# A hybrid of scans, attention and mixtures: image 2's preparation beside image 3's first mixture, and scores without row maxima

## The chip, the cores and the metric

The kernel runs on one core of one Trainium2 chip, in one launch. The metric is the device time of that launch in microseconds (us). Engine names are those of the profile: PE is TensorE (matmuls), PEld its weight loads, DVE is VectorE, ACT is ScalarE, POOL is GpSimd, SP is SyncE, which here issues nearly all DMAs.

## The reference, cut to what matters

Four images of 32 x 32 positions (L = 1024 tokens) with C = 256 channels go through four layers.

```python
# layer 0: norm, project to 512, 3x3 depthwise conv, gelu, then a selective scan with N = 64 states
h = exp(dt[..., None] * A) * h + (dt * x)[..., None] * B[:, None, :]    # for each token in turn
y = einsum("bdn,bn->bd", h, C)
# layer 1: 1x1, grouped 3x3, 1x1 convolutions with a skip
# layer 2a: attention, 8 heads of 32, with a mask from edge_index
scores = where(mask, Q @ K.T / sqrt(32), -inf); attn = softmax(scores); out = attn @ V @ Wo + bo
# layer 2b: mixture of 8 experts (256 -> 256 -> 256), the top 2 of each token
# layer 3a: norm, project, silu, a selective scan with N = 16 states, gate, W_out
# layer 3b: mixture of 8 experts (256 -> 512 -> 256)
top2_vals, top2_idx = top_k(softmax(x @ gate_w + gate_b), 2)
out = sum over e of cw[:, e] * (gelu(x @ W1[e] + b1[e]) @ W2[e] + b2[e])
```

## The kernel before, in words

**Scans.** A scan works in units: one unit is 128 partitions (4 states of 32 channels) by 1024 tokens. There are 256 units an image in layer 0 and 64 an image in layer 3, 1280 in all, in the order (layer, image) = (0,0), (0,1), (3,0), (0,2), (0,3), (3,1), (3,2), (3,3). Each unit loads a tile of dt from memory (`dA<-dt`, 512 KB, on SP's queue, five buffers), takes its exponential on ACT, gets B spread over the partitions by two PE matmuls (`ps_rep`), multiplies on DVE (1.211 us), runs the scan instruction on DVE (2.284 us), multiplies by C on POOL, and is summed by PE (`ps_y`).

**Pacing.** Each engine carries out its instructions in the order in which the program wrote them. The program writes the units' instructions one half unit after another, and between them (`run`, `advance`) as many steps of the other work, a "side", as an estimate allows. `Metered` (line 138 is its `run`, hence the line of nearly every instruction in the profile) adds an estimated cost for each instruction to a clock of each engine, with `matmul_us` for matmuls; side steps are written as long as no engine's clock is ahead of VectorE's, at most two for each half unit. So a changed estimate moves instructions even where nothing else changes.

**Sides.** For each image the side is: the front of layer 0 (beside an earlier scan), then `middle` (the back of layer 0, layer 1, attention, the layer-2 mixture, the front of layer 3), then `last` (the back of layer 3 with `back3`, and the layer-3 mixture `moe(3, ...)`). Attention of one image runs beside the scan of another: image 3's runs beside (3,1) and (3,2).

**Attention.** `heads` works in 64 steps an image: (half of the queries, pair of heads, 128 keys). A step's `scores` are three kinds of matmul into the same PSUM tile `ps_sc`: the products kT by qT, then `onesb` (ones, 32 partitions) by `mT`, then the identity by `maskT`; ACT takes the exponential, and `values` multiplies it by v and by ones (the sums). `mT` holds, for each query and head, minus a row maximum. It is zero unless a bound on the scores, worked out in `attention`, is too large for the exponential: then the rarely taken branch of `shift` works the maxima out with `row_max`. When a group of heads is finished (four times an image), `divided` divides by the sums: DVE takes the reciprocal, POOL multiplies.

**The last layer's mixture.** Image 0's is dense. Images 1 to 3 are sorted: `moe(3, b, ...)` normalizes, routes, ranks the tokens by expert, scatters them (16 indirect DMAs on POOL) into piles of 256 rows in memory, and leaves; `piles` works all piles through (for each, `gx` transposes, `ps_h`, `ps_e`, and a store to `results`), and `gathered` collects each token's two rows and adds them to the image's running sum `tb`. Each image's preparation is `back3` (gate, the projection `ps_o` by W_out into `tb`) and the routing.

**Their places.** Three helpers set the order, and they are what the change touches. `beside(main, other)` writes one step of `other` after each step of `main`. `first_sorted` prepares image 1 beside image 3's layer-2 mixture, yields END, and later, as `self.other` in `last`, works through the piles. `rest` finishes what `other` has left up to END, and only then comes `front3` of image 3, ahead of the scan (3,3). `then_sorted` prepares image 2 and then image 3; `favour` mixes it with the piles, so image 2's preparation is written among the units of (3,3), and what of image 3's follows its scan stands behind the last unit.

Of the kernel before, what the change touches and what calls it, by code (L numbers as in the profile page):

```python
# [9 lines left out]
F32 = mybir.dt.float32  # L10
# [74 lines left out]
def matmul_us(out, lhsT=None, rhs=None, **_):  # L85
    if lhsT is None:
        lhsT = out
    us = 0.46e-3 * columns(out)
    if lhsT.dtype != BF16:
        us = max(4 * us, 0.3)  # L90
    if out.shape[0] <= 32:
        return us / 4
    return us / 2 if lhsT.shape[0] <= 32 else us


def by_columns(per, fixed, of=0):
# [53 lines left out]
class Hybrid:  # L150
# [1154 lines left out]
    def attention(self, b, tb):  # L1305
        nc, tc, vec = self.nc, self.tc, self.vec
        with tc.tile_pool(name=f"at{b}", bufs=1, side="right") as op:
            xa = op.tile([P, TB, C], F32, name="xa")
            qT = op.tile([P, 2, L], F32, name="qT")
            kT = op.tile([P, 2, L], F32, name="kT")  # L1310
            v = op.tile([P, TB, C], F32, name="v")
            mT = op.tile([P, 2, L], BF16, name="mT")
            maskT = op.tile([P, TB, L], BF16, name="maskT")
            wo = self.weight(op, "L2_attn_Wo", 2)
            large = op.tile([1, 1], I32, name="large")
            nc.vector.memset(mT, 0.0)
            with tc.tile_pool(name=f"aa{b}", bufs=1, side="right") as fp:
                wq, wk, wv = (self.weight(fp, "L2_attn_" + n, 2) for n in ("Wq", "Wk", "Wv"))
                xT = fp.tile([P, 2, L], F32, name="xTa")
                yield from self.norm(fp, tb, TB, xa, "lnt")  # L1320
                yield from self.turned(xa, TB, xT)

                def project(item):
                    w, dst, bias, sc, c, g = item
                    ps = self.ps("ps_qk")
                    cols = slice(g * 512, (g + 1) * 512)
                    self.mm(ps, lambda k: w[:, k, c * P : (c + 1) * P], xT, 2, cols)
                    nc.scalar.activation(
                        dst[:, c, cols], ps, AF.Identity, bias=bias[:, c : c + 1], scale=sc
                    )  # L1330

                yield from self.pipe(
                    [
                        (w, dst, bias, sc, c, g)
                        for w, dst, bias, sc in (
                            (wq, qT, self.bq, self.isq), (wk, kT, vec["L2_attn_bk"], 1.0)
                        )
                        for c in range(2) for g in range(2)
                    ],
                    project, cost=1.7,  # L1340
                )

                yield from self.large_scores(fp, qT, kT, large)
                for _ in self.mask_work:
                    pass
                nc.sync.dma_start(maskT, self.mem[("maskT",)].rearrange("j p f -> p j f"))

                def values(j):
                    ps = self.ps("ps_v", (P, 2, C))
                    for i in range(2):  # L1350
                        m = 2 * j + i
                        for k in range(2):
                            nc.tensor.matmul(
                                ps[:, i, :], lhsT=xT[:, k, m * P : (m + 1) * P], rhs=wv[:, k, :],
                                start=(k == 0), stop=(k == 1),
                            )
                    nc.scalar.copy(v[:, 2 * j : 2 * j + 2, :], ps)

                yield from self.pipe(range(TB // 2), values, cost=1.7)
            go = nc.values_load(large, engines=self.sides, min_val=0, max_val=1)  # L1360
            tc.mark_branch_hint_location(f"large{b}", go, engines=self.sides)
            yield from self.add_rows(xa, self.bo, TB)
            yield from self.add_rows(tb, self.beta, TB)
            with tc.tile_pool(name=f"ab{b}", bufs=1, side="right") as fp:
                yield from self.shift(fp, qT, kT, mT, maskT, go, f"large{b}")
            with tc.tile_pool(name=f"ac{b}", bufs=1, side="right") as fp:
                yield from self.all_heads(b, fp, tb, qT, kT, v, maskT, mT, xa, wo)

    def all_heads(self, b, fp, tb, qT, kT, v, maskT, mT, xa, wo):
        nc = self.nc  # L1370

        def divided(raw, sums, c):
            nc.vector.reciprocal(sums[:, c, :], sums[:, c, :])
# [8 lines left out]
            [fp.tile([P, 2, 512], F32, tag=t, name=t, bufs=2) for t in ("raw", "sums")]  # L1382
            for _ in range(2)
        ]
        scores, values = self.heads(fp, halves, qT, kT, v, maskT, mT)
        for n in range(len(steps) + 2):
            if n >= 2:
                values(steps[n - 2])
                yield 1.3
            if n < len(steps):  # L1390
                scores(steps[n])
                yield 1.3
            if then:
                more = next(then[0], None)
                if more is None:
                    then.pop(0)
                else:
                    yield more
            nh, hp, kb = steps[n - 2]
            if n >= 2 and kb == TB - 1 and hp % 2:  # L1400
                then.append(divided(*halves[nh], hp // 2))
                if nh == 0 and hp == 3:
                    then.append(self.finished(b, fp, tb, 0, halves[0][0], xa, wo, "s"))
# [40 lines left out]
        nc.vector.tensor_copy(large, most[:, 0:1])  # L1444
        yield 0.5

    def shift(self, fp, qT, kT, mT, maskT, go, label):


        nc, tc = self.nc, self.tc  # L1450
        clock = dict(self.clock)
        with tc.If(go, preferred_fallthrough_block=True, label=label):
            for _ in self.row_max(fp, qT, kT, mT, maskT):
                pass
        self.clock.update(clock)
        yield 1.0

# [58 lines left out]

        yield from self.pipe([(c, g) for c in range(2) for g in range(2)], turn, cost=0.8)

    def heads(self, fp, halves, qT, kT, v, maskT, mT):

# [4 lines left out]
        def scores(step):  # L1527
            nh, hp, kb = step
            qs = slice(nh * 512, (nh + 1) * 512)
            c, at = hp // 2, 64 * (hp % 2)  # L1530
            alone = self.alone
            if alone:
                both = self.scan_psum.tile([P, 2, 512], F32, tag="x", name="ps_sx", bufs=2)
                two = [both[:, i, :] for i in range(2)]
# [3 lines left out]
            for i in range(2):  # L1538
# [1 line left out]
                    two[i], lhsT=kT[rows[i], c, kb * P : (kb + 1) * P], rhs=qT[rows[i], c, qs],  # L1540
                    start=True, stop=False,
                )
            for i in range(2):
                nc.tensor.matmul(
                    two[i], lhsT=self.onesb[rows[i], :], rhs=mT[rows[i], c, qs],
                    start=False, stop=False,
                )
# [113 lines left out]
                self.router[which].rearrange("p k e -> p (k e)"), ps[:, : 2 * NEXP]  # L1661
            )

    def moe(self, which, b, tb, side="right", stack=None):

        nc, tc, a = self.nc, self.tc, self.a
        w1, w2, b1, hidden = (
# [6 lines left out]
        with ExitStack() as own:  # L1674
# [2 lines left out]
            xT = None if few else xp.tile([P, 2, L], F32, name="xTm")  # L1677
            cw = xp.tile([P, TB, NEXP], F32, name="cw")
            weights, op = {}, None
            spots = self.spots(xp) if few else None  # L1680

            def expert_weights(e):
                we1 = op.tile([P, 2, hidden], F32, tag="we1", name="we1", bufs=2)
# [431 lines left out]
    def gathered(self, b):  # L2115

        nc = self.nc
        tb, _, slot, share = self.sorted_of[b][:4]
        results, got = self.mem["results", b], {}

        def gather(j):
# [316 lines left out]
    def middle(self, b):  # L2438

        with self.tc.tile_pool(name=f"t{b}", bufs=1, side="right") as tp:  # L2440
# [3 lines left out]
            if b < NB - 1:  # L2444
                yield from self.attention(b, tb)
                yield from self.moe(2, b, tb)
            else:
                yield from self.attention(b, tb)
                self.other = self.first_sorted()
                yield from self.rest((yield from self.beside(self.moe(2, b, tb), self.other)))  # L2450
            yield from self.front3(b, tb)

    def some(self, other, n):
        for _ in range(n):
            yield next(other)

    def beside(self, main, other, begin=lambda: True):

        held = None
        for cost in main:  # L2460
            yield cost
            if other is None or not begin() or (held and held not in self.done):
                continue
            held = None
            more = next(other, END)
            if more is END:
                other = None
            elif isinstance(more, Wait):
                held = tuple(more)
            else:  # L2470
                yield more
        if held:
            yield Wait(held)
        return other
# [7 lines left out]
    def first_sorted(self):  # L2482

        with ExitStack() as stack:
            tb = self.scan_pool.tile([P, TB, C], F32, tag="rows", name="tb_rows", bufs=2)
            yield from self.back3(SORTED, tb, "left")
            yield from self.until("route", NB - 1)
            yield from self.moe(3, SORTED, tb, "left", stack)
            yield END
            op = stack.enter_context(self.tc.tile_pool(name="piles", bufs=1, side="left"))  # L2490
            yield from self.piles(op)
# [1 line left out]

    def then_sorted(self):

        with ExitStack() as stack:
            for b in range(SORTED + 1, NB):
                pool = stack.enter_context(self.tc.tile_pool(name=f"e{b}", bufs=1, side="right"))
                tb = pool.tile([P, TB, C], F32, name="tb")
                yield from self.back3(b, tb)  # L2500
                if b == NB - 1:
                    self.gather_pool = stack.enter_context(
                        self.tc.tile_pool(name="found", bufs=1, side="right")
                    )
                yield from self.moe(3, b, tb, "right", stack)
            while "written" not in self.passed:
                yield 0.0

# [77 lines left out]
```

## Time and profile before

Three runs took 6139.52, 6158.01 and 6163.36 us; the median is 6158.01. The profiled execution took 6153.73 us, with a span of 6152.0 us in the profile.

| stretch (us from the span's start) | what runs |
|---|---|
| 0 to 124 | set-up, front of layer 0 of image 0 |
| 124 to 5293 | the scans (0,0) to (3,2), one after another, about 1.3 us apart |
| 1430 to 1679, 2493 to 2740, 3859 to 4117, 4903 to 5149 | the heads of images 0 to 3, each beside a scan |
| 5002 to 5293 | scan (3,2), 291.6 us |
| 5293 to 5522 | no scan: rest of image 3's layer-2 mixture, with image 1's routing; front of (3,3); 228.6 us |
| 5523 to 5861 | scan (3,3), 337.7 us, beside the piles and image 2's preparation |
| 5861 to 6152 | tail, 291.3 us: end of image 3's preparation, the other piles, the gathers |

How to read it: a stretch's bound is the engine whose busy time fills the stretch, or the wait that ends last in it. The total busy share of an engine is an average over all of them. Matmuls on different row groups overlap, so a mean duration times a count can be more than the busy time.

### The profile page before, as it was taken

What the parts mean: (1) busy time and instruction counts of PE and PEld (TensorE: products, weight loads), DVE (VectorE), ACT (ScalarE), POOL (GpSimd) and SP (SyncE); (2) the same over time, 40 slices, a digit from 0 to 9 for tenths busy, and PEclk for the clock granted to TensorE, in tenths of its full rate; (3) what the DMA queues carried; (4) which work ended last, traced back from release to release, by engine and by line L of the source; (5) the groups of instructions that cost most, each with busy time, mean ns of one, the idle gap of its engine ahead of it and who ended that gap; (6) DMA issues with size and microseconds to landing.
All of it is one profiled execution on the core that took longest, in us unless ns stands there. A gap on an engine that the chain in (4) does not pass through costs nothing. (4 is left out here: it accounts for less than half of the span.)

```text
span 6152.0 us, 58992 instructions
## 1 busy us (share of the span) xinstructions
PE 4839.5 (79%) x19373; PEld 1936.7 (31%) x19373; DVE 5037.2 (82%) x4022; ACT 3253.7 (53%) x4225; POOL 3889.2 (63%) x2016
## 2 busy tenths in 40 slices
PE   6676777579979657988868987988865797887787
PEld 2121221032234203224414533224311322543476
DVE  5869798998899899889988998888989888526822
ACT  3455566335568534557754764557753455236431
POOL 1778677766577765657786775657786666306523
PEclk7686877579979757998977988988975897888798
DMA  3665555644345556634554564434555666238656
GB/s 110 187 189 174 155 173 161 201 140 145 124 144 194 164 185 160 162 119 150 198 177 153 173 209 138 133 115 149 197 181 163 164 159 170 74 103 220 175 179 190
DMA packets 396351, 993.17 MB, mean 161 GB/s; under 512 B 42020, under 2 KB 162417, under 8 KB 394417
## 3 DMA queue, kind: packets, MB, share of 16 engines
q1 hardware_dynamic: 388544, 973.48, 52.3%
q0 software_dynamic: 6896, 15.25, 0.9%
q8 instruction: 160, 2.62, 0.2%
q14 instruction: 175, 1.43, 0.1%
q10 hardware_dynamic: 576, 0.39, 0.0%
HBM read 869.33 MB, written 122.26 MB: 161 GB/s over the span
## 5 line engine op out<-in xcount | busy, mean ns | idle before, releaser
L138 POOL TENSOR_TENSOR h<-h,rows 128x1024 f32<-128x1024 f32 x1280 | 3030.0, 2371 | 1685.9 <-DVE h L138 1433.0
L138 DVE TENSOR_TENSOR_SCAN h<-dA,ps_rep 128x1024 f32<-128x1024 f32 x1280 | 2923.7, 2284 | 208.6 <-ACT dA L138 82.6
L138 DVE TENSOR_TENSOR ps_rep<-ps_rep,rows 128x1024 f32<-128x1024 f32 x1280 | 1549.8, 1211 | 205.4 <-PE ps_rep L138 195.3
L138 PE MATMUL ps_rep<-S,spread_L_conv_A_log 96*128 96x512 bf16 x2048 | 769.1, 466 | 843.3 <-DVE h L138 791.8
L138 ACT ACTIVATE dA<-dA,A_L_conv_A_log 128x1024 f32<-128x1024 f32 x1024 | 1126.4, 1143 | 531.9 <-DMA dA<-dt 502.6
L138 PE MATMUL ps_y<-h,collect_L_conv_A_log 128*32 128x512 f32 x4096 | 733.2, 761 | 37.2 <-POOL h L138 36.7
L138 PEld LDWEIGHTS <-spread_L_conv_A_log 96*128 96x128 bf16 x2048 | 159.6, 103 | 1651.5 <-DVE h L138 1329.2
L138 PE MATMUL ps_e<-we,h_m 128*128 128x256 f32 x2112 | 494.7, 385 | 9.0 <-ACT h_m L138 8.2
L138 ACT ACTIVATE p<-ps_sc 128x512 f32<-128x512 f32 x512 | 277.9, 594 | 405.1 <-PE ps_sc L138 400.3
L138 PEld LDWEIGHTS ps_e<-we,h_m 128*128 128x128 f32 x2112 | 402.2, 192 | 115.0 <-ACT h_m L138 25.5
L138 ACT ACT_TABLE_LOAD x326 | 418.3, 1283 | 21.1 <-DMA dA<-dt 15.1
L138 PE MATMUL ps_h<-xTm,we 128*128 128x512 f32 x768 | 366.3, 607 | 0.1
L138 ACT ACTIVATE dA<-dA,A_L_attn_A_log 128x1024 f32<-128x1024 f32 x256 | 283.1, 1144 | 143.4 <-DMA dA<-dt 122.2
L138 PE MATMUL ps_rep<-S,spread_L_attn_A_log 96*128 96x512 bf16 x512 | 182.6, 445 | 171.8 <-DVE h L138 145.1
L138 PE MATMUL ps_sc<-qT,kT 32*128 32x512 f32 x1024 | 310.3, 656 | 5.7 <-ACT p L138 2.4
L138 PE MATMUL ps_at<-p,v 128*32 128x512 f32 x1024 | 273.2, 614 | 0.0
L138 PE MATMUL ps_at<-p,ones 128*32 128x512 f32 x1024 | 273.2, 614 | 0.0
L138 PE MATMUL ps_cv<-pad,diag 128*128 128x512 f32 x504 | 235.1, 607 | 0.0
L138 PEld LDWEIGHTS ps_y<-h,collect_L_conv_A_log 128*32 128x32 f32 x4096 | 96.2, 119 | 376.4 <-issue 226.2
L138 ACT ACTIVATE h_m<-ps_h,cols 128x512 f32<-128x512 f32 x192 | 128.0, 686 | 145.5 <-PE ps_h L138 144.1
L138 PEld LDWEIGHTS ps_h<-xTm,we 128*128 128x128 f32 x768 | 144.0, 192 | 161.3 <-issue 114.8
L138 PE MATMUL ps_y<-h,collect_L_attn_A_log 128*32 128x512 f32 x1024 | 173.5, 693 | 16.7 <-POOL h L138 16.7
(393 smaller groups left out, 5551.6 us busy)
## 6 DMA issues: line engine op xcount, KB each, us to landing
dA<-dt SPq DMA_DIRECT2D x1280, 512.0 KB
we<-in_L_ffn_W_dram SPq DMA_DIRECT2D x88, 512.0 KB
parts<-parts SPq DMA_DIRECT2D x60, 384.0 KB
S<-parts SPq DMA_DIRECT2D x90, 256.0 KB
dt<-sp_r SPq DMA_DIRECT2D x64, 256.0 KB
y<-yo SPq DMA_DIRECT2D x128, 128.0 KB
y_back<-y SPq DMA_DIRECT2D x64, 256.0 KB
we<-in_L_ffn_w_dram SPq DMA_DIRECT2D x64, 256.0 KB
```

Source lines behind the costliest of these rows:

```text
L138: return got(*args, **kw)
```

## The change

It has two parts.

First, the scores lose their `mT` product: 512 matmuls `ps_sc<-mT,onesb` and as many weight loads go, and so do the four memsets of `mT`. The rare case is now worked out as a whole inside the rarely taken branch (`shifted`): all heads with `mT`, stored to memory. After each finished group of heads, `replace` puts a branch on SP that, if the case was taken, loads the stored sums in place of the new ones; otherwise nothing is loaded. `matmul_us` now counts 5/8 where it counted 1/2 for matmuls of 32 input partitions that are not bf16: two such products (0.589 each) are estimated as the two products and two `mT` products were (0.471 and 0.118 each).

Second, `first_sorted` goes on, after image 1, to image 2's `back3` and routing, ahead of END. `beside` may write two steps of the other work for each step of image 3's layer-2 mixture (`most=2`). Image 2's sum `tb` is stored to memory and read back in `gathered`. `then_sorted` prepares image 3 alone.

In the built program the main path has, besides that, 16 more switches on SP, 16 more jumps on every other engine, 12 more table loads on ACT (420 to 432), and a store and a load of image 2's sum on SP. Three quarters of image 3's `ps_o` now stand ahead of the end of its scan, where none of them did.

```diff
@@ matmul_us
-    return us / 2 if lhsT.shape[0] <= 32 else us
+    if lhsT.shape[0] <= 32:
+        return us / 2 if lhsT.dtype == BF16 else us * 5 / 8
+    return us
@@ attention
-            mT = op.tile([P, 2, L], BF16, name="mT")
...
-            nc.vector.memset(mT, 0.0)
...
-                yield from self.shift(fp, qT, kT, mT, maskT, go, f"large{b}")
+                yield from self.shifted(b, fp, qT, kT, v, maskT, go, f"large{b}")
@@ all_heads
+        go = nc.sync.value_load(large, min_val=0, max_val=1)
+
+        def replace(nh, c):
+            for arm in tc.Switch({SP: go}, 2):
+                if arm == 1:
+                    for kind in range(2):
+                        nc.sync.dma_start(
+                            halves[nh][kind][:, c, :], self.mem["large", b, nh][kind, :, c, :]
+                        )
...
             if n >= 2 and kb == TB - 1 and hp % 2:
+                replace(nh, hp // 2)
                 then.append(divided(*halves[nh], hp // 2))
@@ shifted (was shift): inside the rarely taken branch
+            mT = fp.tile([P, 2, L], BF16, name="mT")
+            nc.vector.memset(mT, 0.0)
             for _ in self.row_max(fp, qT, kT, mT, maskT):
                 pass
+            half = [fp.tile([P, 2, 512], F32, name=t) for t in ("raw_l", "sums_l")]
+            scores, values = self.heads(fp, (half, half), qT, kT, v, maskT, mT)
+            for nh in range(2):
...
+                for kind in range(2):
+                    nc.sync.dma_start(self.mem["large", b, nh][kind], half[kind])
+            nc.vector.memset(qT, 0.0)
@@ heads, scores
-            for i in range(2):
+            for i in range(2 if mT is not None else 0):
                 nc.tensor.matmul(
                     two[i], lhsT=self.onesb[rows[i], :], rhs=mT[rows[i], c, qs],
@@ gathered
+        if ("sum", b) in self.mem:
+            tb = self.gather_pool.tile([P, TB, C], F32, name="tb_sum")
+            nc.sync.dma_start(tb, self.mem["sum", b])
@@ middle
-                yield from self.rest((yield from self.beside(self.moe(2, b, tb), self.other)))
+                yield from self.rest((yield from self.beside(self.moe(2, b, tb), self.other, most=2)))
@@ beside: up to `most` steps of other for each step of main
-            more = next(other, END)
...
+            for _ in range(most):
+                if other is None or not begin() or (held and held not in self.done):
+                    break
+                held = None
+                more = next(other, END)
...
@@ first_sorted
             yield from self.moe(3, SORTED, tb, "left", stack)
+            for b in range(SORTED + 1, NB - 1):
+                pool = stack.enter_context(self.tc.tile_pool(name=f"s{b}", bufs=1, side="left"))
+                spots = self.spots(pool)
+                with self.tc.tile_pool(name=f"e{b}", bufs=1, side="left") as pool:
+                    tb = pool.tile([P, TB, C], F32, name="tb")
+                    yield from self.back3(b, tb, "left")
+                    yield from self.moe(3, b, tb, "left", None, spots)
+                    self.nc.sync.dma_start(self.keep(("sum", b), [P, TB, C]), tb)
             yield END
@@ then_sorted: image 3 only
-            for b in range(SORTED + 1, NB):
...
```

More of the change, by code (lines that the diff above doesn't have):

```diff
@@ L1364, in attention, with all_heads @@
             with tc.tile_pool(name=f"ab{b}", bufs=1, side="right") as fp:
[L1365 removed]
+                yield from self.shifted(b, fp, qT, kT, v, maskT, go, f"large{b}")
             with tc.tile_pool(name=f"ac{b}", bufs=1, side="right") as fp:
[L1367 to L1370 removed]
+                yield from self.all_heads(b, fp, tb, qT, kT, v, maskT, xa, wo, large)
+    def all_heads(self, b, fp, tb, qT, kT, v, maskT, xa, wo, large):
+        nc, tc = self.nc, self.tc
+        SP = mybir.EngineType.SP
+        go = nc.sync.value_load(large, min_val=0, max_val=1)
[6 more added lines that the diff above has]
+                        )
         def divided(raw, sums, c):
@@ L1384, in all_heads @@
         ]
-        scores, values = self.heads(fp, halves, qT, kT, v, maskT, mT)
+        scores, values = self.heads(fp, halves, qT, kT, v, maskT)
         for n in range(len(steps) + 2):
@@ L1445, in large_scores, with shifted @@
         yield 0.5
-    def shift(self, fp, qT, kT, mT, maskT, go, label):
+    def shifted(self, b, fp, qT, kT, v, maskT, go, label):
         nc, tc = self.nc, self.tc
         clock = dict(self.clock)
+        for nh in range(2):
+            self.keep(("large", b, nh), [2, P, 2, 512])
         with tc.If(go, preferred_fallthrough_block=True, label=label):
+            mT = fp.tile([P, 2, L], BF16, name="mT")
+            nc.vector.memset(mT, 0.0)
             for _ in self.row_max(fp, qT, kT, mT, maskT):
                 pass
+            half = [fp.tile([P, 2, 512], F32, name=t) for t in ("raw_l", "sums_l")]
+            scores, values = self.heads(fp, (half, half), qT, kT, v, maskT, mT)
+            for nh in range(2):
+                steps = [(nh, hp, kb) for hp in range(4) for kb in range(TB)]
+                for n in range(len(steps) + 1):
+                    if n < len(steps):
+                        scores(steps[n])
+                    if n:
+                        values(steps[n - 1])
+                for kind in range(2):
+                    nc.sync.dma_start(self.mem["large", b, nh][kind], half[kind])
+            nc.vector.memset(qT, 0.0)
         self.clock.update(clock)
@@ L1517, in row_max, with heads @@
         yield from self.pipe([(c, g) for c in range(2) for g in range(2)], turn, cost=0.8)
-    def heads(self, fp, halves, qT, kT, v, maskT, mT):
+    def heads(self, fp, halves, qT, kT, v, maskT, mT=None):
         nc = self.nc
@@ L1530, in scores @@
             c, at = hp // 2, 64 * (hp % 2)
-            alone = self.alone
+            alone = self.alone and mT is None
             if alone:
@@ L1662, in prepare_moe, with moe @@
             )
-    def moe(self, which, b, tb, side="right", stack=None):
+    def moe(self, which, b, tb, side="right", stack=None, spots=None):
         nc, tc, a = self.nc, self.tc, self.a
@@ L1679, in moe @@
             weights, op = {}, None
-            spots = self.spots(xp) if few else None
+            if few and spots is None:
+                spots = self.spots(xp)
             def expert_weights(e):
@@ L2455, in some, with beside @@
             yield next(other)
-    def beside(self, main, other, begin=lambda: True):
+    def beside(self, main, other, begin=lambda: True, most=1):
         held = None
@@ L2461, in beside @@
             yield cost
-            if other is None or not begin() or (held and held not in self.done):
-                continue
-            held = None
-            more = next(other, END)
[L2466 to L2471, printed above, removed]
+            for _ in range(most):
[3 more added lines that the diff above has]
+                more = next(other, END)
+                if more is END:
+                    other = None
+                elif isinstance(more, Wait):
+                    held = tuple(more)
+                else:
+                    yield more
         if held:
@@ L2494, in then_sorted @@
     def then_sorted(self):
+        b = NB - 1
         with ExitStack() as stack:
-            for b in range(SORTED + 1, NB):
[L2498 to L2505, printed above, removed]
+            pool = stack.enter_context(self.tc.tile_pool(name=f"e{b}", bufs=1, side="right"))
+            tb = pool.tile([P, TB, C], F32, name="tb")
+            yield from self.back3(b, tb)
+            self.gather_pool = stack.enter_context(
+                self.tc.tile_pool(name="found", bufs=1, side="right")
+            )
+            yield from self.moe(3, b, tb, "right", stack)
             while "written" not in self.passed:
```

## The prediction

> **What bounds the kernel now.** I read the page first, its busy times and its slices, then busy time by stretch, then the waits inside the stretches that the change touches. On the page:
>
> ```profile
> PE 4839.5 (79%) x19373; PEld 1936.7 (31%) x19373; DVE 5037.2 (82%) x4022; ACT 3253.7 (53%) x4225; POOL 3889.2 (63%) x2016
> ...
> PE   6676777579979657988868987988865797887787
> ...
> DVE  5869798998899899889988998888989888526822
> ...
> PEclk7686877579979757998977988988975897888798
> ```
>
> VectorE has the most work, and holds 8 or 9 tenths wherever a scan runs. But the slices trade places: where PE shows 9, VectorE falls to 8, and in the last seven slices VectorE falls to 2. So the bound changes by stage. The windows give the stages: an attention window (image 0's heads; the others, from 2493.4, 3858.8 and 4903.1, have PE busy 243.1, 255.0 and 243.0 us), the gap between image 2's and image 3's last scans, the last scan, and the tail.
>
> ```profile
> core 0: us, PE busy (x) PEld busy (x) DVE busy (x) ACT busy (x) POOL busy (x), PEclk, DMA share, GB/s
> 1430.30:1678.60 248.30, 245.07 (x1389) 65.07 (x1390) 215.84 (x137) 141.90 (x209) 150.80 (x69) 0.98 0.41 130
> 5293.10:5521.70 228.60, 201.97 (x690) 115.82 (x688) 58.41 (x166) 73.02 (x112) 18.10 (x17) 0.94 0.26 80
> 5523.00:5860.70 337.70, 239.75 (x976) 131.72 (x974) 254.25 (x209) 184.51 (x232) 215.25 (x121) 0.81 0.77 201
> 5860.70:6122.00 261.30, 233.52 (x1092) 195.79 (x1092) 47.17 (x123) 78.07 (x161) 58.56 (x56) 0.93 0.60 187
> ```
>
> In the heads PE is 99% busy and VectorE 87%: PE is the bound there, though a scan runs. In the gap and in the tail it is PE again. In the last scan it is VectorE, with the DMA share at 0.77. The waits of VectorE in image 0's heads agree: it waits for the scan's own matmuls, which stand behind the attention's in PE's order.
>
> ```profile
> DVE ps_rep L138 <- PE ps_rep L138: 13.7, 14, 4.4
> DVE lny_w L138 <- ACT lny_r L138: 7.5, 2, 7.0
> DVE h L138 <- ACT dA L138: 5.5, 13, 0.7
> ```
>
> **Part one: the scores without row maxima.** The group by shape gives what leaves PE:
>
> ```profile
> L138 PE MATMUL ps_sc<-mT,onesb 32*128 32x512 bf16 x512 | 109.3, 383 | 0.0
> ```
>
> 512 matmuls cost 109.3 us together, 0.213 us each, since two row groups overlap (383 ns is one alone); 128 an image, 27.3 us. Image 0's heads keep 245.1 - 27.3 = 217.8 us of PE, against 215.8 us of VectorE: the two become equal. VectorE's idle in the four windows is 32.5, 30.1, 41.4 and 30.0 us, and no window can get shorter than VectorE's work, so 27.3 a window is the ceiling, 109 in all. The estimates that pace the scan's units against the attention do not change (two times 0.471 plus two times 0.118 us before, two times 0.589 after), so both engines keep their order and each half unit still hands over between two engines of equal load. The waits for PE alone are 13.7, 11.2, 22.2 and 11.3 us, 58.4 in sum; those on ACT and on the layer norm stay. I take 49 for those, and 3 for the four memsets of mT on VectorE (3.6 us): **-52**. Bounds -30 (half the waits come back) and -100 (PE's whole cut).
>
> One thing argues for less than the ceiling: the clock. It is 0.98 where PE is 99% busy and 0.82 in 5001.5 to 5293.1, where PE is busy 82%. If PE's share falls to some 94% (217.8 of 233), a clock between them, 0.93, stretches 217.8 us to 217.8 x 0.98 / 0.93 = 230 us, which leaves 248 - 230 = 18 us or less a window; the -13 a window that I take lies below that. [...]
>
> The new branch on SP stands four times an image, 16 in all, between a finished group of heads and its division. Queued behind it on SP is the next dA load, and VectorE's reciprocal of sums waits for it. For the load: SP waits about 208 of 260 us in these stretches for VectorE, and dA lies some 14 us (median) before its use, so a few us are hidden. For the reciprocal: in VectorE's order it stands 1, 2, 4 and 0 units of 3.5 us behind the issue of the branch, so one of the four has no slack. Before has no switch on SP; the nearest row is POOL's in the mask scatter, which takes 0.5 to 2.4 us to compare and 2.5 to 3.9 us until what follows its jump. I charge 2 us an image: **+8**; bounds 0 and +28 (7 us an image, all exposed).
>
> **Part two: image 2's preparation, into the gap.** The gap runs from the end of image 2's last scan, 5293.1, to the first unit of image 3's, 5521.7. It holds the second-layer mixture of image 3 (PE without a break to 5415), then the front of its last scan. VectorE's waits show that it has nothing else to do:
>
> ```profile
> DVE sp_e L138 <- ACT sp_l L138: 81.2, 1, 81.2
> DVE tb L138 <- PE ps_e L138: 60.2, 27, 5.6
> ```
>
> Since PE ends it, what enters PE lengthens it. Image 2's preparation, by the rows of image 1 and image 3: 64 ps_o (15.9 us in the tail), 16 transposes 2.4, 32 logits 3.6, ranks 2.1, weights turned 1.2, biases 4.5: 29.7 us. The extra steps also push the mixture back: 12 of its ps_h (5.6 us) ran under the scan before and no longer do: 35.3. On top are waits that PE takes in order: the layer norm of image 2 (the row of the like in front3 is 7.5 us; I take 6 for both rounds), ranks 4 (the row "PE ps_rk <- DVE bothb" is 4.4), and the weights of the later experts, which SP issues behind image 2's store to its piles, which waits for image 1's 16 scatters on POOL (20.3 us in 5349.6 to 5369.9): I take 10. **+55**. Bounds +36 (PE's work alone) and +85 (every such wait exposed: 7.5 twice, 4.4, and 20.3 for the scatters, 39.7; and some 10 for the second train of scatters, ahead of front3's loads). In the scan before it, 5001.5 to 5293.1, four bias sums and some matmuls leave: **-5**, bounds 0 and -10. ACT gets 12 table loads of 1.283 us, 15.4 us, in the gap, where it is busy 73 of 228.6 us: hidden; if they stood in the chain of norms, some 4 of them would, 5 us, within the bound.
>
> **What it takes from the last scan.** VectorE there has 254.3 us of work; its waits by cause are ACT dA 27.1, PE ps_rep 21.7, ACT sp_l 17.4. Image 2 takes away some 25 us of it (adds of ps_o 2.7, norm 6.5, routing 10 to 14, ranks 5.5, bias sums 2.8), and three of image 3's four partial adds come in, 2.1. But more piles are put there (10 before, 16 after, by the order written into the changed kernel), each 6.9 us of PE and ACT beside the scan, and the DMA share is already 1.03 in 5600 to 5700. I credit a bit over half of the 23 us: **-14**, bounds 0 and -40.
>
> **The tail.** From 5860.7 PE works through piles. The chain shows one pile as a ps_h and a ps_e:
>
> ```profile
> 6082.63 3.46 PE ps_h L138 x16
> 6086.09 3.45 PE ps_e L138 x16
> 6089.98 3.46 PE ps_h L138 x16
> ```
>
> 6089.98 - 6082.63 = 7.35 us a pile. Before leaves 26 piles there, after 20: 6 x 7.35 = 44. Image 3's output projection leaves 64 ps_o, 15.9 us; after leaves a quarter: 12. That is 56 of PE's 233.5 us; 27.8 us of the window are idle, much of it around image 3's chain, which comes some 25 us earlier, so 7 more go. The last gathers stay, about 30 us, with image 2's sum now read back from memory (0 to 3). **-63**, bounds -45 and -70.
>
> **Sum.** -52 + 8 - 5 + 55 - 14 - 63 = **-71**. The profiled execution took 6153.73 us (span 6152.0), so 6083; the median of the three runs is 4.3 above it, so **6087**.
>
> **The rivals.**
> 1. *The heads get PE's whole cut*: -100 in place of -52, so 6039. For it: no wait of VectorE's but PE's is long there. Against: the loads are then equal to 1%, and two engines in order never fit that well.
> 2. *The clock takes the heads' gain.* PE at 0.98 needs 217.8 us; it fills the old 248 at 217.8 x 0.98 / 248 = 0.86, which is near the 0.82 seen at 82% busy. Then 0 in place of -52: 6139. Against: a slower clock fills PE's share up again, and at 99% it was 0.98.
> 3. *The jumps cost on all engines.* Each of the 16 switches puts a jump on every engine. If one costs VectorE or PE the middle of POOL's 2.5 to 3.9 us, 16 x 3.2 = 51 in place of 8: 6130. Against: in the mask scatter VectorE runs over its jumps with no gap to be seen. [...]
> 4. *Slower: image 2's chain is not hidden beside the mixture.* Place: the gap. SP's store for image 2 waits for image 1's scatters, the experts' weights wait behind it, PE in order behind them, and front3's weights wait for image 2's scatters. Price: image 3's same chain takes 151 us in the tail, from the scan's end to its routing branch at 6012; with two trains of scatters, 2 x 20.3, the gap grows by 192 and not by 55: +66, so 6224. It decides from a growth of 126 us (no change), 157 for a slowdown that can be told. For it: one queue serves all loads. Against: image 1's same preparation, beside the same mixture, left PE one stall of a few us.
>
> That image 2's preparation does not move is excluded by the order written into the changed kernel, where all its ps_o stand ahead of front3.
>
> **How the numbers follow.** A measurement of this kernel can tell about 0.5%, 31 us, from no change (the three runs span 24). Forecast 0.56, rivals 1 to 4: 0.15, 0.10, 0.06, 0.13. The forecast's own bounds, taken as independent (up: 22, 20, 5, 30, 14, 18; down: 48, 8, 5, 19, 26, 7; roots of the sums of squares 49 and 59), give 6028 to 6136. The range reaches up to rival 2 and part of the way to rival 4: 6026 to 6155. Faster by over 0.5% means below 6127: 0.51 of the forecast, rival 1, half of rival 3, 0.01 of rival 2: 0.70. Slower: 0.12 from rival 4. The same: the remaining 0.18.
>
> **What would show it.** In the heads, four windows of about 235 us, with PE's share under 99%, the waits for ps_rep halved, and the granted clock read off directly (rival 2: below 0.88). VectorE's reciprocal of sums waiting for SP under 3 us (rival 3: gaps of some 3 us after jumps, 16 times on an engine). The gap 270 to 300 us (rival 4: above 360, with PE waiting on DMA we). The last scan some 324 us; the tail about 228 us with 20 piles. Wrong it would be if the gap took back more than the tail and the last scan return, 77 us, or if the heads kept their length.

## The result, and the profile after

The changed kernel took 6099.87 us (median; 6090.8 to 6102.72) against 6151.74 for the kernel before beside it: a ratio of 0.9902, with a 95% interval of 0.9874 to 0.9931. Measured again beside other kernels it was 0.9907 (0.9885 to 0.9929). That is about 1% faster: 52 us between the medians, 60 by the ratio of 0.9902 (on 6158), where 71 were forecast. The profiled execution had a span of 6100.0 us, 52.0 less than the profile before. From its page, the busy times and the slices:

```profile
PE 4760.5 (78%) x18773; PEld 1906.7 (31%) x18861; DVE 5025.3 (82%) x4018; ACT 3262.5 (53%) x4237; POOL 3888.5 (64%) x2016
...
PE   5676777578979757888967987988865797787786
...
DVE  5869798998889899888988998889989899525742
...
PEclk8686867579979857897977998988975898888898
```

PE lost 79.0 us of busy time, VectorE 11.9. Some 13 of the 79.0 are no time saved: 88 of the 512 mask matmuls have no record in the profile after (18773 matmuls against 18861 weight loads; 19373 of both before), and in their place PE shows 13.4 us of idle time with no wait behind it. VectorE's row ends in 5 2 6 8 2 2 before and in 5 2 5 7 4 2 now: the gap is longer, and the tail, in which VectorE has little to do, shorter. The same four stretches as before, in the same columns (us, busy time and count of PE, PEld, DVE, ACT, POOL, granted clock, DMA share, GB/s):

```profile
1429.90:1670.50 240.60, 231.47 (x1239) 59.32 (x1262) 214.45 (x137) 140.57 (x209) 150.19 (x69) 0.96 0.41 133
5246.50:5548.10 301.60, 256.42 (x891) 150.69 (x890) 80.48 (x239) 88.51 (x136) 48.79 (x45) 0.88 0.29 92
5548.10:5860.20 312.10, 245.02 (x1040) 151.67 (x1041) 232.75 (x143) 206.85 (x262) 191.80 (x97) 0.89 0.88 228
5860.20:6070.00 209.80, 178.94 (x851) 148.25 (x850) 44.26 (x118) 60.64 (x125) 52.53 (x51) 0.93 0.58 185
```

The heads of image 0 take 240.6 us in place of 248.3, the gap 301.6 in place of 229.9 (counted here to the next unit's scan instruction, 1.3 us behind its first), the last scan 312.1 in place of 337.7, the tail 239.8 in place of 291.3 (its last 30 us, the gathers, are not in the row). VectorE's waits in image 0's heads are still led by the scan's matmuls:

```profile
DVE ps_rep L140 <- PE ps_rep L140: 11.2, 6, 4.7
DVE lny_w L140 <- ACT lny_r L140: 5.9, 1, 5.9
DVE h L140 <- ACT dA L140: 1.8, 4, 0.7
```

One profile of each kernel is not enough for terms of 10 us. The table sets the stages of all runs side by side; rows with the same placing of a stage and the same estimate agree within some 12 us. The tails of the first pair are the exception, and on both sides: 291.3 before, where three other kernels with the same tail have 303 to 309, and 239.8 after, where the others have 253 to 261. With the estimate at 1/2 the gaps are shorter (284.0 and 214.1).

| kernel | end of (3,2) | gap | last scan | tail | ratio to before (95%) |
|---|---|---|---|---|---|
| before | 5293.1 | 229.9 | 337.7 | 291.3 | 1 |
| after | 5246.5 | 301.6 | 312.1 | 239.8 | 0.9902 (0.9874 to 0.9931) |
| after, again | 5260.8 | 298.8 | 308.4 | 252.8 | 0.9907 (0.9885 to 0.9929) |
| part one alone | 5257.9 | 241.4 | 340.6 | 308.8 | 0.9930 (0.9910 to 0.9950) |
| part two alone | 5269.2 | 303.1 | 304.3 | 261.3 | 0.9962 (0.9944 to 0.9979) |
| after, no branches on SP | 5246.1 | 302.9 | 303.8 | 256.3 | 0.9896 (0.9870 to 0.9922) |
| before, mT pairs doubled | 5352.3 | 233.1 | 342.2 | 307.6 | 1.0102 (1.0075 to 1.0129) |
| after, one step beside | 5249.2 | 303.4 | 308.2 | 256.0 | 0.9917 (0.9890 to 0.9943) |
| after, three steps late | 5255.1 | 291.7 | 306.1 | 258.4 | 0.9895 (0.9869 to 0.9922) |
| the same, again | 5249.2 | 289.3 | 302.0 | 260.7 | 0.9890 (0.9866 to 0.9915) |
| after, estimate 1/2 | 5304.6 | 284.0 | 308.1 | 256.0 | 0.9965 (0.9950 to 0.9981) |
| after, estimate 3/4 | 5250.0 | 304.8 | 298.1 | 261.2 | 0.9913 (0.9890 to 0.9936) |
| part one alone, estimate 1/2 | 5318.9 | 214.1 | 343.0 | 303.0 | 1.0012 (0.9999 to 1.0025) |

### The profile page after: what moved, and what is told of

It is laid out like the page before. It is cut to its first block, busy times and chain, and to the rows that moved or that the text cites. A ratio compares the mean times of both kernels' runs of the same rounds, so it can differ in the third digit from the quotient of the medians.

```text
span 6100.0 us, 58148 instructions
## 1 busy us (share of the span) xinstructions
PE 4760.5 (78%) x18773; PEld 1906.7 (31%) x18861; DVE 5025.3 (82%) x4018; ACT 3262.5 (53%) x4237; POOL 3888.5 (64%) x2016
## 3 DMA queue, kind: packets, MB, share of 16 engines
q14 instruction: 230, 1.88, 0.1%
## 5 line engine op out<-in xcount | busy, mean ns | idle before, releaser
L140 PE MATMUL ps_h<-x,we 128*128 128x256 f32 x576 | 161.1, 435 | 35.3 <-ACT h_m L140 14.0
## 6 DMA issues: line engine op xcount, KB each, us to landing
S<-parts SPq DMA_DIRECT2D x90, 256.0 KB
dt<-sp_r SPq DMA_DIRECT2D x64, 256.0 KB
we<-in_L_ffn_w_dram SPq DMA_DIRECT2D x64, 256.0 KB
y_back<-y SPq DMA_DIRECT2D x63, 256.0 KB
```

Of the source, the lines that this page charges most:

```text
L140: return got(*args, **kw)
```

## The experiments

**Part one alone.** The diff without the hunks from `moe` on.

> Part one alone: no mT products, the new branches on SP, the changed estimate; image 2's preparation stays in the last scan. Theory A (the price of a pair of mT matmuls is the step that it adds between the starts of its neighbours, 0.742 - 0.527 = 0.215 us, 55 us in all, and the heads stay bound by PE): about 42 us faster than before, the four heads windows near 240 us, gap 5293 to 5522 and tail as long as before. Rival B (part two gives some of the gain: 22 us as predicted): about 30 us faster. Rival C (the shorter scan (3,2) in the changed kernel, 8 us, comes from part two): 34 us faster.

Measured: 0.9930 of a median of 6176.8, 43 us faster (31 to 56). That is theory A's 42; B's 30 lies just outside the interval and C's 34 just inside. The four heads windows are 240.7, 245.1, 243.4 and 237.6 us, near A's 240. Scan (3,2) took 286.3 us (from the end of the scan before it) against 284.6 in the changed kernel, 292.9 before and 289.6 in part two alone. So most of its gain goes with part one, which speaks against C; one profile of each is not proof.

**Part two alone.** The kernel before with the hunks from `moe` on.

> Part two alone: image 2's preparation beside image 3's first mixture, with the mT products kept. Theory A (the gap grows by some 73 us, which takes back what the last scan, 26, and the tail, 52, return): 5 us faster than before, within 10. Rival B (the prediction's terms: gap +55, last scan -14, tail -63, scan before -5): 27 us faster. The gap's growth tells: 73 or 55.

Measured: 0.9962, 23 us faster (13 to 35). That is B's total, and not A's: the single pair of profiles, from which A's 5 us were taken, misled. Gap, last scan and tail add up to 858.9 us in the profile before, but to 890.8 and 882.9 in part one alone and in the kernel with doubled pairs, which have the same placing; part two alone has 868.7, and the changed kernel without its branches 863.0. Why the profile before was so much shorter here is not known. But the gap grew as A said: 303.1. The total comes from larger terms on both sides.

**The branches left out.**

```diff
-        go = nc.sync.value_load(large, min_val=0, max_val=1)
...
-                replace(nh, hp // 2)
```

> The changed kernel without the 16 branches on SP (left out: the loads of the replacement sums in the rare case, which these inputs don't take). Theory A (the branches cost next to nothing; VectorE waited for SP once, 1.0 us): within 4 us of the changed kernel, 0.990 of before. Rival (2 us an image as predicted, or up to 7): 8 to 28 us faster than the changed kernel, 0.986 to 0.989 of before.

Measured: 0.9896 (0.9870 to 0.9922), against 0.9902 and 0.9907 with the branches: theory A, no price that can be seen, though an interval of 16 us to each side could not tell the 8 us from nothing. The four heads windows sum to 961.7 us without the branches and to 960.5 and 973.5 with them.

On SP itself the branches do take time. In the changed kernel SP's next instruction starts 2.8 to 7.8 us (median 4.0) after the jump of each switch; behind SP's ten branches in the kernel before it is 0.12 to 0.46 us. SP has that time to spare: it comes out of its waits for VectorE. From 1430 to 1700, with four branches, then without:

```profile
SPq L509 <- DVE h L140: 188.5, 55, 9.7
SPq L509 <- DVE h L140: 206.5, 57, 9.7
```

VectorE waits for SP once in the whole changed kernel, for 1.0 us. Behind its own 16 jumps VectorE idles 0.7 us four times and otherwise not at all.

**The mT pairs doubled.**

```diff
-            for i in range(2):
-                nc.tensor.matmul(
-                    two[i], lhsT=self.onesb[rows[i], :], rhs=mT[rows[i], c, qs],
+            for i in range(4):
+                (nc if i < 2 else nc.what).tensor.matmul(
+                    two[i % 2], lhsT=self.onesb[rows[i % 2], :], rhs=mT[rows[i % 2], c, qs],
```

> The kernel before with each pair of mT matmuls issued twice (mT is zero here, so the sum stays), not counted in the estimates, so that nothing else moves. Theory A (a pair adds the step between starts, about 0.22 us, 256 pairs): PE's bound in the heads grows by 14 us a window, 55 us in all, 0.9% slower. Rival (the price of the row of the profile, 0.213 us each, 0.427 a pair): 27 us a window, 109 in all, 1.8% slower. If VectorE and not PE set the heads: no change.

Measured: 1.0102, 63 us slower (46 to 80): theory A's 55 lies inside the interval, the row's 109 and the third case, no change, outside. The four heads windows grew from 998.6 to 1065.8 us. Where the price lies is seen in the starts of the matmuls. First one step of the scores in the profile before, then one after (timeline of PE: start, length, name, count):

```profile
1503.11 1.13 PE L138 MATMUL ps_sc<-qT,kT 32*128 32x512 f32 x4
1504.07 0.38 PE L138 MATMUL ps_sc<-mT,onesb 32*128 32x512 bf16 x2
1504.38 0.60 PE L138 MATMUL ps_sc<-maskT,identb 128*128 128x512 bf16 x2
```

```profile
1502.29 1.13 PE L140 MATMUL ps_sc<-qT,kT 32*128 32x512 f32 x4
1503.35 0.61 PE L140 MATMUL ps_sc<-maskT,identb 128*128 128x512 bf16 x2
```

From the first product to the mask's it is 1504.38 - 1503.11 = 1.27 us before and 1.06 after. Over all 256 pairs of the heads windows the medians, from the third of the four qT products to the first mT product and from there to the mask's, are 0.429 + 0.313 = 0.742 before; from the third qT product straight to the mask's it is 0.527 after. In the doubled kernel the step from the first mT product to the mask's is 0.530 in place of 0.313, 0.217 more for the second pair. So a pair was worth 0.215 us, 55 us in all, and not the 0.427 that the busy time gives it. Without it, the step from the 32-row products to the 128-row mask is longer than the step to mT was (0.527 against 0.429): what came free was partly a step that has to be made anyway.

**One step beside the mixture.**

```diff
-                yield from self.rest((yield from self.beside(self.moe(2, b, tb), self.other, most=2)))
+                yield from self.rest((yield from self.beside(self.moe(2, b, tb), self.other, most=1)))
```

> The changed kernel, but with one step of the other work for each step of the mixture, as before: image 1's preparation takes the mixture's steps, and image 2's comes after it, alone. Theory A (image 2's chain costs little only because the mixture covers it; alone it takes what image 3's takes in the tail, some 70 us to its ranks, and more to the end): the gap grows by 100 to 130 us over before in place of 68, total 30 to 60 us above the changed kernel, 0.995 to 1.000 of before. Rival (the gap's growth is PE's work, order does not matter): within 8 us of the changed kernel.

Measured: 0.9917, within 10 us of the changed kernel, with a gap of 303.4: the rival's total is right, and theory A falls. The mixture ends at 5383, 134 us after the scan, and then image 2 stands alone on PE:

```profile
5383.11 13.98 PE L140 MATMUL ps_o<-w_L_attn_W_out,y_back 128*128 128x256 f32 x64
5404.64 5.62 PE L140 MATMUL ps_tr<-ident,xnm 128*128 128x128 f32 x16 [7.55 <-ACT xnm L140]
5410.05 6.83 PE L140 MATMUL ps_lg<-wr,xTm 128*128 128x8 f32 x32
...
5423.43 1.87 PE L140 MATMUL ps_ct<-ident,cw 128*8 128x128 f32 x8
5425.22 7.19 PE L140 MATMUL ps_b<-b,cT 8*128 8x256 f32 x16
5455.20 5.62 PE L140 MATMUL ps_tr<-ident,xn 128*128 128x128 f32 x16 [22.79 <-ACT xn L140]
```

From 5383 to 5432 image 2 takes 49 us, and front3's transposes start 23 us later: 72 us, as much as the gap grows with everything interleaved. PE is idle more here (7.6 + 22.8 us at the two norms, before image 2's transposes and before front3's), but busy less, 244.1 us of the gap in place of 256.4. Of these 12.3 us, 11.9 are ps_h: 115 of them stand in this gap (57.1 us), 128 in the changed kernel's (69.0 us). With one step beside it the mixture begins its ps_h under the scan, as before; with two it is pushed back behind the scan's end. So what the interleaving saves in waits goes to matmuls that it moves into the gap. In the 72 us PE is busy for only 36.4, so the rival's reason, PE's work alone, is only half of it. PE was busy in nearly all of the mixture before (119.8 of the 122.0 us from 5293 to 5415), so its own work for image 2 could hide nowhere.

**Three steps, late.**

```diff
-                yield from self.rest((yield from self.beside(self.moe(2, b, tb), self.other, most=2)))
+                yield from self.rest((yield from self.beside(self.moe(2, b, tb), self.other, most=lambda: 3 if "first" in self.passed else 1)))
...
             yield from self.moe(3, SORTED, tb, "left", stack)
+            self.passed.add("first")
```

(In `beside`, `most` is called if it can be.)

> The changed kernel, with one step beside each step of the mixture until image 1 is prepared and three after. Theory A (cover counts): between the run with one step and the changed kernel, the gap grows by 85 to 110 us over before, but its first 50 us run as before, with the granted clock near 1.0 in place of 0.56 to 0.87, which gives back some 10. Rival (the low clock at the gap's start is what costs): faster than the changed kernel by 10 us.

> The version with one step beside the mixture until image 1 is prepared and three after, which had the shorter gap (292 and not 302 us): if the gap's 10 us are real and nothing else pays for them, 10 us faster than the changed kernel on the same chip, 0.987 to 0.989 of before; if they are the scatter of one profile, within 4 us of it.

> The changed kernel again, on the same chip as the next one. If its two parts add up, part one 43 us and part two 23: 0.988 to 0.990 of before. If its first measurement, 0.9902, was low by chance in either direction, this tells.

Measured: 0.9895 and, again, 0.9890, with gaps of 291.7 and 289.3; the changed kernel on the same chip as the second was 0.9907. The medians differ by 17.8 us (6104.05 and 6121.86), the gaps by 10; the intervals overlap, so this version is the best that ran, without being shown to beat the changed kernel. Theory A's growth of the gap by 85 to 110 us did not come (62 and 59). The changed kernel's 0.9907 lies just above the 0.988 to 0.990 expected of two parts that add up. The start of the gap differs as expected. In the changed kernel, two stretches from 5246:

```profile
5246.00:5256.00 10.00, 8.62 (x22) 3.92 (x21) 3.62 (x8) 1.87 (x2) 2.34 (x1) 0.61 0.29 78
5256.00:5266.00 10.00, 10.00 (x27) 5.32 (x26) 3.58 (x15) 4.30 (x7) 0.00 (x0) 0.87 0.11 28
```

In the late version, the first of its gap:

```profile
5249.20:5262.00 12.80, 12.47 (x46) 7.18 (x45) 5.22 (x16) 2.55 (x4) 2.35 (x1) 1.00 0.16 41
```

The late version begins the gap at a granted clock of 1.00: expert matmuls already run under the scan's end, and PE has no pause above 1 us from 5207 to 5275. The changed kernel has two pauses of 5.0 us shortly before the gap (they end at 5229 and 5237), begins it at 0.61, and 16 ps_h take 9.1 us there (5254.6 to 5263.7) in place of some 7. The clock is not the whole of the 10 us: the late version also has 115 ps_h in its gap and not 128, which is some 6 us at 0.457 each.

**The estimate.** The line of `matmul_us`, in the changed kernel with 1/2 and with 3/4, and in part one alone with 1/2.

```diff
-        return us / 2 if lhsT.dtype == BF16 else us * 5 / 8
+        return us / 2
```

> The changed kernel with the old estimate (1/2 and not 5/8): the heads are written beside 53 units of the scan and not 58. Theory A (the heads stay bound by PE, at 98% of the window, and VectorE idles some 20 us in each): VectorE idles 9 us more in each of four windows, which later units do not give back; the last image's mixture comes 5 units earlier, which gives 10 back: 15 to 25 us slower than the changed kernel, 0.993 to 0.994 of before. Rival (VectorE has become the bound, as in the prediction's two equal loads): within 5 us.

> Part one alone, but with the old estimate (1/2): the mT products go and the heads are written beside 53 units in place of 58. Theory A (the changed kernel lost 38 us with the old estimate, in the scans; the pacing, not the matmuls, decides whether part one pays): part one's gain of 43 us shrinks to some 5, 0.998 to 1.000 of before. Rival (that loss belongs to part two, for example to where image 3's mixture begins): the gain stays above 30 us, 0.995 or less.

> The changed kernel with a larger estimate (3/4 and not 5/8): the heads are written beside 63 units and not 58. Theory A (heads bound by PE): each window's VectorE idle falls by 8 us for images 0 to 2, 24 in all, and image 3's mixture comes some units later, which costs 5 to 15: 10 to 20 us faster than the changed kernel, 0.987 to 0.988 of before. Rival (two equal loads: what VectorE gains in the windows it loses in units that came later): within 5 us.

Measured: 0.9965, some 38 us slower than the changed kernel; for part one alone 1.0012, just above A's 0.998 to 1.000, so its gain is gone (theory A in both, and more than its 15 to 25 us in the first). With 3/4 it is 0.9913, no gain: the rival. The windows of image 0's heads show why. With 1/2 in the changed kernel, then with 3/4:

```profile
1425.00:1658.00 233.00, 228.43 (x1235) 57.81 (x1236) 197.72 (x126) 134.28 (x202) 138.99 (x64) 0.97 0.40 126
```

```profile
1426.70:1681.80 255.10, 245.21 (x1295) 60.30 (x1296) 230.71 (x147) 145.15 (x213) 161.53 (x74) 0.95 0.44 137
```

With 1/2 the window holds 53 units in place of 58 and is 233.0 us long, 15.3 less than before. But the five units that left are 5 x 3.495 = 17.5 us of VectorE, done elsewhere: nothing is gained. With 5/8 the 58 units stay, and the window still shortens by 7.7. Against the changed kernel with 5/8, the four windows with 1/2 are 24.8 us shorter in sum, but 20 units, 69.9 us of VectorE, have left them: 45 us lost, near the 38 measured. With 3/4 there are 63 units and 255.1 us: 14.5 more than with 5/8, for 17.5 of scan; image 3's window, 266.6 us against 240.5, takes that back.

## Why the prediction was right, and where its terms were off

**The total and its sign held**, and so did the split: part one was put at -44 with the branches, part two at -27 with the -5 in scan (3,2). The runs give -43 and -23. That the total came so near was partly luck. By stages, as given below, the terms missed by +14 (heads), -8 (branches), -3 (scan (3,2), 8 us shorter), +12 (gap), -19 (last scan) and +13 (tail), and these cancel to +9. (The upper of the two roots behind the bounds is 48 and not 49, which changes nothing.)

**The heads: the size of the cut was wrong.** The step "512 matmuls cost 109.3 us together" took busy time for a price. The cut was 55 us. So the ceiling was half of what the prediction had, rival 1 (-100) could not have happened, and the -52, about half of my ceiling, would have been nearly all of the real one. The four windows fell from 998.6 to 960.5 us in the first pair of profiles (38), and to 959.7 to 973.5 in the other kernels with part one and 5/8; part two alone, which keeps the mT products, has 992.6. What did not come through in the first pair lies in PE. Its idle time in the four windows grew by 14 us (12.4 before; 39.6 after, less the 13.4 of the missing records); half of that is its waits for ACT's p (9.5 us for the scores, 2.4 before). And it ran 64 us of the windows at a clock of 0.50, 56 before, which costs 4 us by an estimate: half of the 8, since four `ps_h` of the gap take 1.88 us at 1.00 and 3.78 at 0.50 (at 5266.95 and 5274.27). The -52 rested on VectorE's waits for PE, 58.4 us, and those fell only to 43.1; that it came within 14 us was partly luck.

**The clock.** It was 0.96 in image 0's heads, 0.98 before, and 0.97 in the others, which had 0.99, 0.94 and 0.99. I had put 0.93, by a line between the rows at 99% and at 82% of PE. That mechanism was wrong: taken in shorter stretches, the granted clock of these traces is 0.50 or 1.00 and nothing between, and the figure of a window is the mix. Image 0's heads in the changed kernel:

```profile
1430.00:1439.00 9.00, 8.27 (x20) 2.12 (x22) 4.68 (x3) 2.17 (x4) 8.36 (x5) 0.50 0.40 134
1439.00:1602.70 163.70, 157.07 (x869) 40.87 (x882) 147.74 (x99) 98.50 (x144) 94.99 (x42) 1.00 0.41 133
1602.90:1613.00 10.10, 10.10 (x31) 1.94 (x34) 9.65 (x6) 4.12 (x8) 7.74 (x4) 0.50 0.49 156
1613.20:1670.50 57.30, 55.58 (x325) 14.26 (x324) 52.07 (x30) 35.78 (x53) 38.67 (x19) 1.00 0.41 131
```

PE is busy all through the second slow stretch, so the clock does not follow the busy share of the moment. That stretch stands right behind a pause of PE of 2.24 us (it waits for the scan, up to 1602.31). In the eight heads windows, before and after, five slow stretches lie behind the first 20 us; four of them stand right behind such pauses, of 1.9 to 2.2 us, and five like pauses have none behind them. What makes the clock fall is not shown here. Rival 2 is out.

**The branches** were charged with 8 us; the runs show none. SP does lose 2.8 to 7.8 us at each, more than POOL's 2.5 to 3.9 that I went by, but this is hidden in SP's waits. My two readings for that slack were loose: the 208 us of waits are those of image 0's window alone (178.7 and 129.2 in images 1 and 3), and the 14 us before dA's use count from the issue of the load, its transfer included. Rival 3 is out: behind their 16 jumps VectorE idles 2.8 us in sum and PE 2.3. What holds SP behind its jumps no run here shows.

**The gap: +55, measured some +67** (229.9, 241.4 and 233.1 with the old place, 298.8 to 303.1 with the new). The waits came out about as put: PE's idle time grew by some 18 us, forecast 20. PE's busy time grew by 54.5 (201.97 to 256.42) where the sum had 35.3. Over half of what was missed goes with the clock, 0.88 and not 0.94 in the gap: the ps_h of the mixture took 69.0 us in all where 128 at the old 0.457 would be 58.4, that is 11 us. The rows of the gap, before and after:

```profile
L138 PE MATMUL ps_h<-xTm,we 128*128 128x512 f32 x115 | 52.5, 594 | 0.0
L140 PE MATMUL ps_h<-xTm,we 128*128 128x512 f32 x128 | 69.0, 685 | 10.5 <-DMA we<-in_L_ffn_w_dram 7.0 <-ACT h_m L140 2.7 <-DVE tb L140 0.9
```

The wait for the experts' weights, put at 10 and at most 20, was 7.0 (ps_h <- DMA we). So rival 4's mechanism is there, but small: alone, image 2's chain costs 72 us, not 192. I had taken its length from image 3's chain in the tail, where piles stand in PE's order between its steps.

**The last scan: -14, measured some -33** (337.7, 340.6 and 342.2; then 303.8 to 312.1). My credit of a bit over half was too careful: VectorE's busy time fell by 21.5 us (254.25 to 232.75), near the 23 that I had, and all of that came through. The six additional piles hid beside the scan although the DMA share rose to 0.88. (The listed pieces of image 2's work add up to 27.5 to 31.5 us, not to the prediction's 25.) As the scan shortened by more than VectorE's work, some of VectorE's idle time went too; why stays open.

**The tail: -63, measured some -50** (291.3, 308.8 and 307.6; then 239.8 to 261.3). PE's work there fell by 233.5 - 178.9 = 54.6 us, as put (56); the 7 us of waits did not go: PE's idle time is 30.9 us after and 27.8 before. The read-back of image 2's sum, put at 0 to 3, stands in the chain of the changed kernel's tail with 10:

```profile
5981.76 8.13 DMA found<-results,slot x2
5990.94 9.97 DMA tb_sum<-sum
6011.60 4.63 DMA found<-results,slot
```

What the whole would gain without that read-back was not tried.

## What to carry to other kernels

Take the price of a matmul that shares its PSUM tile with neighbours of another shape from the steps between starts, before and (if there is one) in a place without it, and not from its busy time (here 0.215 us a pair, not 0.427). Where two engines share a stretch, the ratio in which their work is written into it is part of the change: the same cut was worth 43 us with the ratio kept, and nothing with five units fewer beside it. A chain that is moved beside an engine already at its bound need not hide there: here the gap grew by some 67 us, and the move paid by what it freed at its old place, some 33 us in the last scan and 50 in the tail.

## What the runs showed of the hardware

A pair of 32-row bf16 matmuls between 32-row and 128-row ones added 0.215 us to the order of PE, with 0.427 us of busy time; without it, the change from 32-row to 128-row matmuls took 0.527 us from start to start. Behind the jump of each of sixteen switches SP stood still for 2.8 to 7.8 us, and VectorE for at most 0.7; the kernel's time showed no cost (0.9896 without them, 0.9902 and 0.9907 with them). The granted clock was 0.50 or 1.00, and means between the two are mixes. At the start of the gap, with PE 62% busy in the 10 us before and 65 to 100% in it, it went back and forth for some 40 us: 0.50 from 5248 to 5258, from 5272 to 5279 and from 5286 to 5289, 1.00 between and after these (0.61, 0.87, 0.81, 0.84, 0.84 in stretches of 10 us from 5246).
